# Moving one tile's layernorm statistics within VectorE's queue, in a two-layer graph network on one core

## The chip, the cores and the metric

The kernel runs on one core of a Trainium2 chip. The metric is the time on the device in microseconds, the median of three runs. The core has five engines that run their own instruction streams side by side: TensorE (PE, matrix products and transposes into PSUM), VectorE (DVE), ScalarE (ACT), GpSimd (POOL), and SyncE (SP), which issues the transfers. Each engine takes its instructions in the order in which they are written, and waits at an instruction until what it needs is ready.

## The reference, cut to what matters

There are 64 graphs of 256 nodes with 512 channels, and a 256 x 256 adjacency for each. Two layers follow one another, each on a normalised copy of x that passes through a relu, and each adds to x:

```python
h = jnp.maximum(_layernorm(x, axis=-1), 0.0)
# layer 0: attention with 8 heads of 64, masked by adj, and a gate
q, k, v = (x @ Wq.T, x @ Wk.T, x @ Wv.T)          # on h, split into heads
attn = softmax(where(adj != 0, q.k / 8, -inf))
c = attn @ v
gate = sigmoid(concatenate([c, h]) @ Wg.T + bg)
x = x + gate * h + (1.0 - gate) * c
h = jnp.maximum(_layernorm(x, axis=-1), 0.0)
# layer 1: graph attention with one head
Wh = h @ W
e = leaky_relu(Wh.a1[:, None] + Wh.a2[None, :], 0.2)
x = x + elu(softmax(where(adj == 0, -1e9, e)) @ Wh)
```

The statistics of the title are the mean and variance over the 512 channels of each node, for layer 0's layernorm.

## The kernel before, in words

**Tiles.** A graph's 256 nodes are two tiles of 128 rows, so x is one tile of 128 x 2 x 512 in float32, and t is 0 or 1 throughout. `norm_stats` (L186) takes the mean and variance of one row tile on VectorE: BATCH_NORM_STATS2 at L191, an aggregate at L192, and after the second tile an addition of epsilon at L195. GpSimd takes the power -1/2 (`norm_root`, L199), VectorE the bias (`norm_bias`, L203), ScalarE normalises (`norm_relu`, L208).

**Products.** All projections and the gate go through seven products of halves instead of eight (`strassen`, L153). Their sums are kept in three PSUM banks, a, b and c. Products 1 and 2 go to bank a; 6, 7 and 4 to b; 5 and 3 to c. Within a bank a product adds to what stands there. In between, the partial sum is read out: `u1` is a copy of bank a on ScalarE (L182); `u2` and `u3` are bank b plus u1 on VectorE (L180), after products 6 and 7; `c00`, `c10`, `c11` and `c01` are the four quarters of the result, of which c00 is ScalarE's and the others are VectorE's. Two facts of this bear on the change: product 4 adds to bank b, so it can't begin until u3 has read it; and the next family of products can't begin in bank b until c10 has read it. In the trace, product 1 of the gate begins with `pma_z<-hT_l,wgh_sb`, and product 4 is the group that begins with `pmb_z<-hT_l,wgh_t`.

**Rounds.** `emit_round(i)` (L607) writes the instructions of one round in a fixed order, by hand; nothing reorders them, and each engine keeps it. A round works on up to five graphs at once: attention of graph i, projections of p = i + 1, gate and layer 1's first half of q = i - 1, layer 1's second half of r = i - 2, and, ahead of these, the mask and statistics of p + 1. The load of x for p + 2 is issued at the end of a round (`load_graph`, L88), on SyncE's queue, after the store of graph r and the transfers of `p_send`; its statistics are taken in the next round, where that graph is p + 1.

**The stretch around the change** is the gate's. TensorE does products 1, 6, 5, two small transposes (`g_edges`, L529, which spread layer 1's edge terms over the rows, into `pe`), then products 7, 2, 4 and 3. VectorE does u2, the reciprocal of a softmax sum (L357), the statistics of tile 0, the logits (L535, two instructions, which read `pe`), the leaky relu (L542, one instruction that reads its tile twice), the row maximum (L544), u3, c11, block transposes of the attention weights (L370), the reciprocal of layer 1's sums (L558), the statistics of tile 1 with L195, c10, and then the gate's mix (`g_mix`, L453 and L455), which waits for ScalarE's tanh (L445), which waits for c10. ScalarE waits for the row maximum to take layer 1's exponential (L551), and then copies c00. GpSimd scales the attention weights (L361), takes the differences d for the gate (`g_diff`, L440, two subtractions), the sums for the projections' products (`p_sums`, L147 to L150) and the root (L199).

Of the kernel before, what the change touches and what calls it, by code (L numbers as in the profile page):

```python
# [22 lines left out]
def kernel(  # L23
# [79 lines left out]
    def weight_sums(key):  # L103

        w = weight[key]
        t = const.tile([P, 3, 2, w.shape[3]], F32, name=f"w{key}_t")
        b11, b12, b21, b22 = (w[:, r:r + 2, n, :] for r in (0, 2) for n in range(2))
        nc.vector.tensor_tensor(t[:, 1], b22, b12, ALU.subtract)
        nc.vector.tensor_tensor(t[:, 0], t[:, 1], b11, ALU.add)
        nc.vector.tensor_tensor(b12, b12, b11, ALU.subtract)  # L110
        nc.vector.tensor_tensor(t[:, 2], b21, t[:, 0], ALU.subtract)
        weight[key] = {1: b11, 2: b21, 3: b22, 4: t[:, 2], 5: b12, 6: t[:, 0], 7: t[:, 1]}
# [10 lines left out]
    def edge_columns():  # L123

        w = weight["1"]
        for c in range(HC):
            for side in range(2):
                scr = sb["tmp"].tile([P, 2, HH], F32, tag="t", name=f"scr_{c}_{side}")
                nc.vector.scalar_tensor_tensor(
                    scr, w[:, c, :, :HH], 1.0, a_sb[side].rearrange("p (n f) -> p n f", n=2),  # L130
                    ALU.mult, ALU.mult, accum_out=w[:, c, side, HH:],
                )
# [474 lines left out]
    def emit_round(i):  # L607


        p, q, r = i + 1, i - 1, i - 2  # L610

        def do(fn, g, *args):
            if 0 <= g < B:
                fn(g, *args)

        def run(fn, g, steps):
            if 0 <= g < B:
                if (fn, g) not in products:
                    products[fn, g] = fn(g)
                for step in steps.split():  # L620
                    products[fn, g](step)

        run(g_gate, q, "1")
        run(g_wh, r, "c01")
        do(a_turn, i, 0, 0)
        do(a_send, i, 0, 0)
        do(p_fetch, p)
        do(a_fetch, i, 0, 0)
        run(g_gate, q, "u1 6 u2 5")
        do(a_scale, i, 0, 1)  # L630
        do(p_stats, p + 1, 0)
        do(g_edges, r)
        do(g_logits, r)
        do(g_leaky, r)
        do(g_diff, q)
        run(g_gate, q, "7 u3 c11")
        do(g_exp, r)
        do(a_turn, i, 0, 1)
        do(a_send, i, 0, 1)
        do(a_fetch, i, 0, 1)  # L640
        run(g_gate, q, "2 c00")
        do(p_sums, p)
        do(g_rec, r)
        do(p_stats, p + 1, 1)
        do(p_root, p + 1)
        run(g_gate, q, "4 c10")
        do(g_tanh, q, 0)
        run(g_gate, q, "3")
        do(g_mix, q, 0, True)
        run(g_gate, q, "c01")  # L650
        do(g_tanh, q, 1)
        do(g_mix, q, 0, False)
        do(g_transpose, r)
        do(g_targets, r)
        do(p_mask, p + 1)
        do(g_mix, q, 1, True)
        do(g_mix, q, 1, False)
        do(g_turn, q)
        do(g_send, q)
        do(g_fetch, q)  # L660
        do(p_bias, p + 1)
        if i == -1:
            weight_sums("q")
            weight_sums("k")
        run(p_qk, p, "1 u1 6 5 u2")
        do(g_out, r, 0)
        do(g_neg, r, 0)
        do(g_pos, r, 0)
        do(a_scores, i, 1)
        do(a_weigh, i, 0)  # L670
        do(a_max, i, 1, 0)
        do(a_exp, i, 1, 0, 0)
        do(a_exp, i, 1, 0, 1)
        do(a_max, i, 1, 1)
        do(a_evac, i, 0)
        run(p_qk, p, "7")
        do(a_exp, i, 1, 1, 0)
        do(a_exp, i, 1, 1, 1)
        do(a_scale, i, 1, 0)
        run(p_qk, p, "u3")  # L680
        do(a_scale, i, 1, 1)
        run(p_qk, p, "c11 2 c00")
        do(a_turn, i, 1, 0)
        do(a_send, i, 1, 0)
        do(g_residual, q)
        do(a_fetch, i, 1, 0)
        run(p_qk, p, "4 c10")
        do(g_stats, q, 0)
        do(g_stats, q, 1)
        do(g_root, q)  # L690
        run(p_qk, p, "3 c01")
        if i == -1:
            weight_sums("v")
        run(p_v, p, "1 u1")
        do(g_bias, q)
        do(g_norm, q)
        run(p_v, p, "6 u2")
        do(g_elu, r, 0)
        do(g_add, r, 0)
        do(a_turn, i, 1, 1)  # L700
        do(a_send, i, 1, 1)
        do(a_fetch, i, 1, 1)
        do(g_out, r, 1)
        run(p_v, p, "5")
        do(g_neg, r, 1)
        if i == 0:
            weight_sums("gh")
            weight_sums("gc")
            nc.vector.tensor_scalar_mul(hbg, hbg, 0.5)
        run(p_v, p, "7 u3")  # L710
        do(g_transpose_h, q)
        run(p_v, p, "2")
        do(g_channels, q)
        run(p_v, p, "c11")
        do(g_sums, i)
        run(p_v, p, "c00")
        do(g_pos, r, 1)
        do(p_norm, p + 1)
        run(p_v, p, "4 c10 3 c01")
        do(g_elu, r, 1)  # L720
        do(g_add, r, 1)
        do(g_store, r)
        do(p_turn, p + 1)
        do(p_send, p + 1)
        do(load_graph, p + 2)
        if i == 0:
            edge_columns()
            weight_sums("1")
        run(g_wh, q, "1 u1 6 u2 5")
        do(a_scores, p, 0)  # L730
        do(a_max, p, 0, 0)
        do(a_exp, p, 0, 0, 0)
        do(a_exp, p, 0, 0, 1)
        run(g_wh, q, "7 2 c00")
        do(a_max, p, 0, 1)
        run(g_wh, q, "u3 c11")
        do(a_scale, p, 0, 0)
        do(a_exp, p, 0, 1, 0)
        do(a_weigh, i, 1)
        do(a_evac, i, 1)  # L740
        do(a_sums, i)
        do(a_exp, p, 0, 1, 1)
        run(g_wh, q, "4 c10 3")

    with tc.manual_schedule(engines={getattr(mybir.EngineType, e) for e in ("PE", "SP", "Pool", "DVE", "Activation")}):
        load_graph(0)
        load_weight("q", nc.sync)
        load_weight("k", nc.scalar)
        load_graph(1)
        load_weight("v", nc.sync)  # L750
        p_mask(0)
        p_stats(0, 0)
        p_stats(0, 1)
        for fn in (p_root, p_bias, p_norm, p_transpose_pe):
            fn(0)
        for i in range(-1, B + 2):
            if i == 0:
                load_weight("gh", nc.sync)
                load_weight("gc", nc.sync)
                load_weight("1", nc.sync)  # L760
                load_small()
            emit_round(i)
            graphs.pop(i - 2, None)
# [32 lines left out]
```

## Time and profile before

| what | value |
|---|---|
| time, median of three | 3369.89 us (3366.17 to 3376.53) |
| span of the profiled run | 3364.0 us, its time 3365.78 us |
| TensorE, busy with matmuls | 3262.3 us, 97% |
| VectorE busy | 2398.4 us, 71% |
| GpSimd busy | 1641.1 us, 49% |
| ScalarE busy | 1369.0 us, 41% |
| granted TensorE clock, mean | 0.991 |
| statistics L191 | 256 instructions, mean 675 ns; VectorE idle 85.9 us before them, for the load of x |

Half of the 256 statistics belong to layer 0, and half of those to tile 0. A line of a group in the page gives line, engine, operation, tiles written and read, shapes, count, then busy time, mean duration in ns, and the time that the engine sat idle ahead of it, with what ended that. A line of the list of waits gives who waited, for whom, the total in us, how often, and the longest. A line of a timeline gives start and duration in us, engine, line of the kernel, operation and tiles, and in brackets the idle time before it and what ended it. The work of a middle round repeats every 50.4 to 51.7 us.

### The profile page before, as it was taken

Reading aid. Unit: us, or ns where it says so; the run is one execution under the profiler, and the core shown is the slowest. Engines: PE = TensorE matmul, PEld = TensorE weight load, DVE = VectorE, ACT = ScalarE, POOL = GpSimd, SP = SyncE. Lnnn points to the kernel's source line nnn. Section 1 sums busy time; section 2 is a strip of 40 time slices with the busy share of each in tenths; the row PEclk is TensorE's granted clock in tenths of the full one; section 3 lists DMA queues with packets and bytes.
Section 4 is the critical chain, followed back from the end, with each engine's and each line's share of the span. In section 5 each row is a group of like instructions: output and inputs, shape, how many; then the busy total and the mean of one; then the engine's idle time right before and its main releaser. Section 6 shows DMA issues by size and latency. Waiting matters only on the chain. (4 is left out here: it accounts for less than half of the span.)

```text
span 3364.0 us, 66545 instructions
## 1 busy us (share of the span) xinstructions
PE 3262.3 (97%) x23448; PEld 2804.2 (83%) x23448; DVE 2398.4 (71%) x6245; ACT 1369.0 (41%) x3843; POOL 1641.1 (49%) x2439
## 2 busy tenths in 40 slices
PE   6999999999999999999999999999999999999996
PEld 5788888888888888888888888888888888888884
DVE  5777777777777776777777777777777777767764
ACT  2344443443443444343444434434444444434342
POOL 2454554544544544545545545445455445445453
PEclk8999999999999999999999999999999999999998
DMA  4455545545545545545545455455455455454541
GB/s 160 139 146 152 152 142 156 157 138 154 157 141 153 162 137 156 154 142 154 146 153 156 138 156 158 138 154 157 136 159 158 139 157 156 142 150 140 152 128 57
DMA packets 614765, 494.61 MB, mean 147 GB/s; under 512 B 291233, under 2 KB 540577, under 8 KB 614433
## 3 DMA queue, kind: packets, MB, share of 16 engines
q1 hardware_dynamic: 613376, 489.31, 49.4%
q8 instruction: 187, 3.06, 0.4%
q14 instruction: 146, 1.19, 0.1%
q10 hardware_dynamic: 1056, 1.05, 0.1%
HBM read 256.90 MB, written 233.31 MB: 146 GB/s over the span
## 5 line engine op out<-in xcount | busy, mean ns | idle before, releaser
L361 POOL TENSOR_SCALAR e<-e,rec 128x256 f32<-128x256 f32 x1024 | 471.4, 479 | 1104.6 <-DVE rec L357 640.4
L349 ACT ACTIVATE e<-e,low 128x256 f32<-128x256 f32 x1024 | 508.0, 499 | 201.9 <-DVE low L340 201.9
L340 DVE CUSTOM_DVE_ANT_0 e<-ps,mask 128x256 f32<-128x256 f32 x1024 | 363.3, 421 | 60.6 <-PE ps L325 60.2
L370 DVE STREAM_TRANSPOSE eb<-e 128x512 f32<-128x512 f32 x512 | 331.9, 686 | 3.5 <-POOL e L361 3.0
L325 PEld LDWEIGHTS ps<-qk 64*128 64x128 f32 x2048 | 187.8, 187 | 86.7 <-issue 69.3
L325 PE MATMUL ps<-qk 64*128 64x256 f32 x2048 | 256.5, 390 | 0.0
L402 PE MATMUL pc<-eT,v 128*64 128x256 f32 x2048 | 249.5, 386 | 0.3 <-DMA eT<-there_e 0.3
L577 PE MATMUL po<-wh,egT 128*128 128x512 f32 x512 | 245.0, 602 | 2.6 <-ACT egT L571 2.6
L551 ACT ACTIVATE eg<-eg,nm 128x256 f32<-128x256 f32 x128 | 64.0, 500 | 450.2 <-DVE nm L544 450.2
L191 DVE BATCH_NORM_STATS2 bs_l<-x 128x6 f32<-128x512 f32 x256 | 172.8, 675 | 85.9 <-DMA x<-in_x_dram 85.9
L208 ACT ACTIVATE h_l<-x,nb_l,rs_l 128x512 f32<-128x512 f32 x256 | 194.3, 808 | 61.8 <-DVE nb_l L203 46.0
L589 ACT ACTIVATE pos<-po,rec 128x512 f32<-128x512 f32 x128 | 88.3, 690 | 321.1 <-DVE neg L584 321.1
L402 PEld LDWEIGHTS pc<-eT,v 128*64 128x64 f32 x2048 | 135.7, 137 | 98.5 <-issue 22.4
L199 POOL TENSOR_TENSOR rs_l<-ve_l,mhalf 128x2 f32<-128x2 f32 x128 | 90.0, 703 | 261.1 <-DVE ve_l L195 258.8
L147 POOL TENSOR_TENSOR S_l<-hT_l 128x256 f32<-128x256 f32 x128 | 93.2, 728 | 238.8 <-ACT hT_l L136 162.4
L599 POOL TENSOR_TENSOR x<-x,pos 128x512 f32<-128x512 f32 x128 | 163.2, 1275 | 93.5 <-DVE pos L595 93.5
L445 ACT ACTIVATE z<-z,hbg 128x256 f32<-128x256 f32 x256 | 116.3, 501 | 222.3 <-DVE z L180 222.3
L349 ACT ACTIVATION_READ_ACCUMULATOR e<-e,low 128x1 f32 x1024 | 193.7, 189 | 0.0
L440 POOL TENSOR_TENSOR d<-hT_l,cT 128x512 f32<-128x512 f32 x128 | 174.5, 1384 | 0.0
L584 DVE TENSOR_SCALAR neg<-po,rec 128x512 f32<-128x512 f32 x128 | 93.4, 730 | 109.3 <-PE po L577 109.3
L180 DVE TENSOR_TENSOR u_qk<-pmb_qk,u_qk 128x512 f32<-128x512 f32 x128 | 87.8, 686 | 105.9 <-PE pmb_qk L169 105.9
L169 PEld LDWEIGHTS pmb_qk<-S_l,wq_t 128*128 128x128 f32 x1024 | 125.3, 193 | 33.5 <-issue 27.0
(144 smaller groups left out, 8235.7 us busy)
## 6 DMA issues: line engine op xcount, KB each, us to landing
there_e<-eb SPq DMA_DIRECT2D x256, 512.0 KB, 2.7
eT<-there_e SPq DMA_DIRECT2D x1024, 128.0 KB, 3.0
x<-in_x_dram SPq DMA_DIRECT2D x64, 512.0 KB, 5.8
out_dram<-x SPq DMA_DIRECT2D x64, 512.0 KB, 3.0
there_y<-y SPq DMA_DIRECT2D x63, 512.0 KB, 2.6
yT<-there_y SPq DMA_DIRECT2D x252, 128.0 KB, 3.0
there_h<-h_l SPq DMA_DIRECT2D x248, 128.0 KB, 3.6
hT_l<-there_h SPq DMA_DIRECT2D x248, 128.0 KB, 5.2
```

What stands on the lines that cost most here:

```text
L169: nc.tensor.matmul(bank[key][(slice(None), *cols)], lhsT, rhs, start=first and i == 0, stop=last and i == len(todo) - 1, skip_group_check= ...
L191: nc.vector.bn_stats(bs, s["x"][:, t, :])
L208: nc.scalar.activation(h[:, t, :], s["x"][:, t, :], AF.Relu, bias=s["nb"][:, t:t + 1], scale=s["rs"][:, t:t + 1])
L325: nc.tensor.matmul(psc[jj, i][:, t, :], qk[r:r + DK, 0, jj, t * P:(t + 1) * P], qk[r:r + DK, 1, jj, :], start=True, stop=True,)
L340: nc.vector.tensor_tensor_reduce(s["e", half, jj][:, i, t, :], s["ps", half][jj, i][:, t, :], s["mask"][:, t, :], -SCALE, HUGE, ALU.add, A ...
L349: nc.scalar.activation(e, e, AF.Exp, bias=s["low", half][:, jj, i, t:t + 1], scale=-1.0, accum_out=s["sums", half][:, jj, i, t:t + 1],)
L361: nc.gpsimd.tensor_scalar(e, e, rec[:, i, t:t + 1], 1.0, ALU.mult, ALU.mult)
L370: nc.vector.transpose(eb[:, :, 4 * i:4 * i + 4, :].rearrange("p b n c -> p n b c"), e[:, i])
L402: nc.tensor.matmul(pc[i * DK:(i + 1) * DK, jj, :].rearrange("p (t a c) -> p t a c", t=NT, c=32), s["v"][:, kc, hd * DK:(hd + 1) * DK], eT[ ...
L440: nc.gpsimd.tensor_tensor(d, s["hT"][:, :, js, :], s["cT"][:, :, js, :], ALU.subtract)
L577: nc.tensor.matmul(pm, s["egT"][:, kc, t * P:(t + 1) * P], s["wh"][:, kc, :, :HH], start=(kc == 0), stop=(kc == NT - 1))
L599: nc.gpsimd.tensor_tensor(s["x"][:, t, :], s["x"][:, t, :], s.pop(("pos", t)), ALU.add)
```

## The change

Within `emit_round` two things change their place, and with them their place in VectorE's queue. The statistics of tile 0 of graph p + 1 stood behind the scaling's reciprocal and ahead of the logits; now they stand behind the block transposes, c00 and layer 1's reciprocal. The gate's `4 c10` stood behind both tiles' statistics and the root; now it stands between the two tiles' statistics. No instruction is added, dropped or altered. Its purpose is that VectorE should not stand before the load of x while the logits and u3 are queued behind it.

```diff
         run(g_gate, q, "u1 6 u2 5")
         do(a_scale, i, 0, 1)
-        do(p_stats, p + 1, 0)
         do(g_edges, r)
         do(g_logits, r)
         do(g_leaky, r)
...
         run(g_gate, q, "2 c00")
         do(p_sums, p)
         do(g_rec, r)
+        do(p_stats, p + 1, 0)
+        run(g_gate, q, "4 c10")
         do(p_stats, p + 1, 1)
         do(p_root, p + 1)
-        run(g_gate, q, "4 c10")
         do(g_tanh, q, 0)
         run(g_gate, q, "3")
         do(g_mix, q, 0, True)
```

## The prediction

> **What bounds the kernel now.** I read the page's table of engines first, then TensorE's list of waits, then the timelines of one long and one short round.
>
> ```profile
> PE 3262.3 (97%) x23448; PEld 2804.2 (83%) x23448; DVE 2398.4 (71%) x6245; ACT 1369.0 (41%) x3843; POOL 1641.1 (49%) x2439
> ...
> L542 DVE SCALAR_TENSOR_TENSOR eg<-eg 128x512 f32<-128x512 f32 x64 | 77.2, 1206 | 2.2
> ```
>
> TensorE has work during 97% of the span, so only what still makes it wait can be won. The second line is put by for later: L542 has a mean of 1206 ns, while the same kind of instruction on the same shape takes 697 ns at L453. The waits of TensorE, with total, count and longest:
>
> ```profile
> PE pmb_z L169 <- DVE u_z L180: 34.8, 31, 2.8
> PE pt_l L268 <- ACT h_l L208: 23.6, 6, 11.7
> PE pmb_z L169 <- POOL S_c L148: 8.1, 1, 8.1
> PE pmb_qk L169 <- POOL S_l L148: 6.3, 1, 6.3
> ```
>
> The last three rows are start and end of the program (few waits, long ones). The first is the only wait of the steady state: 31 of some 60 rounds. The timeline says which u_z it is. First a long round, 51.65 us from one start of the gate's step 1 to the next, that starts at 1523.37 (VectorE, then TensorE, then GpSimd; columns are start, duration, instruction, idle time before it and what ended that):
>
> ```profile
> 1527.20 0.42 DVE L180 TENSOR_TENSOR u_z<-pmb_z,u_z 128x256 f32<-128x256 f32 x1 [1.99 <-issue]
> ...
> 1529.25 0.69 DVE L191 BATCH_NORM_STATS2 bs_l<-x 128x6 f32<-128x512 f32 x1 [1.54 <-DMA x<-in_x_dram]
> ...
> 1530.07 0.84 DVE L535 SCALAR_TENSOR_TENSOR eg<-pe,wh,mask 128x256 f32<-128x256 f32 x2
> 1530.95 1.70 DVE L542 SCALAR_TENSOR_TENSOR eg<-eg 128x512 f32<-128x512 f32 x1
> 1532.69 0.69 DVE L544 TENSOR_REDUCE nm<-eg 128x2 f32<-128x512 f32 x1
> 1533.29 0.41 DVE L180 TENSOR_TENSOR u_z<-pmb_z,u_z 128x256 f32<-128x256 f32 x1
> ```
>
> ```profile
> 1528.73 0.38 PE L529 MATMUL pe<-ident,wh 128*128 128x128 f32 x2
> ...
> 1533.76 1.16 PE L169 MATMUL pmb_z<-hT_l,wgh_t 128*128 128x128 f32 x8 [1.08 <-DVE u_z L180]
> ```
>
> ```profile
> 1529.61 2.50 POOL L440 TENSOR_TENSOR d<-hT_l,cT 128x512 f32<-128x512 f32 x2
> ```
>
> Then a short round, 50.41 us, that starts at 2797.71:
>
> ```profile
> 2802.53 0.69 DVE L191 BATCH_NORM_STATS2 bs_l<-x 128x6 f32<-128x512 f32 x1 [0.49 <-DMA x<-in_x_dram]
> ...
> 2803.49 0.87 DVE L535 SCALAR_TENSOR_TENSOR eg<-pe,wh,mask 128x256 f32<-128x256 f32 x2
> 2804.39 1.37 DVE L542 SCALAR_TENSOR_TENSOR eg<-eg 128x512 f32<-128x512 f32 x1
> ...
> 2806.40 0.41 DVE L180 TENSOR_TENSOR u_z<-pmb_z,u_z 128x256 f32<-128x256 f32 x1
> ```
>
> The reader is to see a chain. The statistics of x (tile 0) wait for the load of x; behind them in VectorE's queue stand the logits, the leaky step L542, the maximum, and then u3, which must read bank b before step 4 may accumulate into it. All further times are counted from the start of step 1 of the round. u3 begins at 9.92 in the long round and at 8.69 in the short one. TensorE reaches step 4 at 9.16 and u3 takes 0.41, so 8.69 is just in time and 9.92 is 1.08 us of idle TensorE.
>
> Between the two rounds nothing else differs on this path, and the delay comes in a **step, not in proportion**: over rounds 1 to 60, L542 that starts at 7.38 or earlier ends at 8.05 to 8.08 (29 rounds), one that starts from 7.45 to 8.36 ends at 9.28 or 9.29 in all but one. Whatever begins in between waits for an edge. GpSimd's two subtractions of L440 run from 6.24 to 7.51 and from 7.47 to 8.74, and these are the edges: L542 takes its 0.69 us in the seam between them, or after the second.
>
> **What the Trainium skill says.** "SBUF — State Buffer", section "Who interferes with whom": a VectorE instruction with two SBUF inputs contends with a GpSimd instruction that reads SBUF, and the shared port pair is held as an exclusive lock for a whole instruction. L542 has two SBUF inputs and L440 reads SBUF; 0.69 us free against up to 1.84 us beside L440 agrees. "Perfetto Trace Analysis", section "Identifying the Most-Contended Engine": busy share of matmuls is a poor measure of the distance to the bound; here too the list of waits told more than the 97%. "TensorE: Matmul & The Clock Gate", section "What's actually happening": a free-running activity window of about 3.4 us decides on half or full clock, and an idle one halves it. In the trace one 3.41 us stretch at half clock begins 0.2 us after the longest wait, and no other in the middle of the program; that wait was 2.75 us, so less than a whole window was enough.
>
> **The change part by part.**
>
> Nothing is added or dropped: 63 BATCH_NORM_STATS2 (0.67 us) and 63 aggregates (0.18 us) of tile 0 move within VectorE's queue, from ahead of the logits to behind the block transposes, c00 and the reciprocal; and c10 moves ahead of the statistics of tile 1.
>
> *Removed ahead of u3.* Two things: the wait for x (85.9 us over 59 waits, mean 1.46) and 0.67 + 0.18 us of work. What then bounds the logits is pe, the two transposes at L529, which end at 5.74 (1529.11 - 1523.37). So logits at 5.78, L542 at 6.69, in every round. This case is in the trace already: rounds 61 and 62 have no statistics of a later graph, their logits start at 5.78, L542 at 6.69 and takes 1.36, and u3 comes at 8.69. L542 at 6.69 lies inside the first subtraction of L440 and well ahead of the 7.4 where the step is, with 0.7 us to spare. Hence u3 at 8.69 always, and no wait at step 4.
>
> *What that is worth.* A long round costs 51.65 - 50.42 = 1.23 us more: 1.08 of wait and 0.15 of restart. 31 waits give 34.8 us, the restarts 31 x 0.15 = 4.7, and the one long wait with its half clock a further 54.95 - 50.42 - 2.75 - 0.15 = 1.6. Sum 41.1; adding up what each of the rounds 1 to 60 has over 50.42 gives 41.0, so I take **41 us**.
>
> *Added behind.* In a short round of before the reciprocal L558 ends at 10.82, then statistics of tile 1, aggregate and the epsilon add L195 (0.17 to 0.45), then c10 from 12.00 to 12.41. After: statistics and aggregate of tile 0 end at about 11.62, c10 runs from 11.66 to 12.07, 0.35 earlier. Step 4 has ended by 11.0, so c10 doesn't wait for it. tanh follows c10 by 0.1 and takes 0.91 for its two: to 13.08. Meanwhile VectorE does tile 1's 0.67 + 0.18 and L195, to 13.1 or 13.4. The mix d (L453) began at 13.51 before, after 1.10 us in which VectorE waited for tanh; that idle time hides the statistics. So the cost is **nothing**, bounded by 0 and by 0.4 us of VectorE that TensorE doesn't wait for.
>
> *The waits that move.* The wait for x stands now at about 10.75. In the trace x came at 8.56 at the latest, so I take zero. Behind it queue c10 (tanh waits for it; so does p_qk's step 6 for bank b, at 15.05, 3 us after c10's end) and, from there on, work for which TensorE shows no wait. GpSimd's root rs_l waits for L195 and moves from 12.2-14.1 to about 13.3; GpSimd's next work behind it is the next scaling, well past 20, and VectorE needs the root (L203) at about 18. The block transposes and their send come no later than in a short round.
>
> **The rivals.**
>
> *A, the forecast:* all rounds short. 3365.8 for the profiled run less 41.0 = 3324.8. The median of before is 4 us above the profiled run, which I put down to some more long rounds; these go too, and I leave 1 us for odd rounds like number 32 (0.37 us). **3326.**
>
> *B, half stays:* u3 at 8.69 leaves no slack (its end at 9.10, step 4 at 9.16). If the lock at L542 or a slip of the later pieces brought the step back in half of the rounds, 3369.9 - 20 = 3350. For it speaks that the margin at step 4 is 0.06 us; against it rounds 44 to 47, four short ones in a row, and rounds 61 and 62.
>
> *C, the wait only changes its place:* c10 or the mix late, bank b or c free late for the projections of q and k. It would take over 3 us at c10 to touch p_qk; then about 3367. Against it: the earlier c10 worked out above.
>
> *D, slower:* the 0.85 us of tile 0 lands whole on the path in its new place, 60 x 0.87 = 52 us against 41 won: 3381. It would need TensorE to wait for d, c01 or y; no row of before has such a wait, and 1.10 us of VectorE idle time stands right there.
>
> **How the numbers follow.** A 0.87, B 0.05, C 0.04, D 0.04. The time is A's. The low end is the floor of 3324.8 less the 0.1% by which runs scatter; the high end takes in B's milder half, a quarter of the loss left with a slow run: 3345. Faster by over 0.3% (below 3359.8): A and B, 0.92; within: C, 0.04; slower: D, 0.04.
>
> **What would show it.** Right: no row of TensorE waiting for u_z at step 4, or a few; VectorE's wait for x gone from L191; logits waiting some 1.4 us for pe instead (1.44 in rounds 61 and 62); L542 near 1.36 us in all middle rounds; rounds at 50.42; d's wait for tanh down from 1.10 to below 0.3 us. Wrong: L542 near 1.7 with u3 at 9.9, a new row of TensorE waiting for z or y, or L191 still waiting for x at its new place.

## The result, and the profile after

The changed kernel takes 3322.99 us (median of four runs, 3321.47 to 3324.14), against 3372.3 us before (3366.17 to 3376.53, four runs; the 3369.89 of the table above is the median of the first three). The ratio is 0.9855, with a 95% interval of 0.9837 to 0.9872: 1.45% faster. The runs also lie closer together, within 2.7 us where the kernel before spread over 10.

The row of the statistics in the page of the kernel before, and then the engines and the same row in the page of the changed kernel:

```profile
L191 DVE BATCH_NORM_STATS2 bs_l<-x 128x6 f32<-128x512 f32 x256 | 172.8, 675 | 85.9 <-DMA x<-in_x_dram 85.9
```

```profile
PE 3255.3 (98%) x23448; PEld 2803.0 (84%) x23448; DVE 2405.5 (72%) x6245; ACT 1369.6 (41%) x3843; POOL 1674.8 (50%) x2439
...
L191 DVE BATCH_NORM_STATS2 bs_l<-x 128x6 f32<-128x512 f32 x256 | 172.2, 673 | 0.0
```

Behind the second bar stands VectorE's idle time ahead of the statistics: 85.9 us before, none now. TensorE's waits, longest in total first:

```profile
PE pt_l L268 <- ACT h_l L208: 23.9, 6, 11.7
PE pmb_z L169 <- POOL S_c L148: 8.3, 1, 8.3
PE pmb_qk L169 <- POOL S_l L148: 6.3, 1, 6.3
```

The row of 34.8 us for u_z is gone, and no new one of that kind has come; what is left belongs to the start and the end. VectorE waits elsewhere, where it costs nothing. One row of before, then two of now:

```profile
DVE d L453 <- ACT z L445: 63.2, 59, 1.5
```

```profile
DVE eg L535 <- PE pe L529: 91.4, 64, 1.5
...
DVE d L453 <- ACT z L445: 5.0, 7, 1.1
```

The logits now wait for pe, 91.4 us in total, about as long as VectorE used to wait for x; the mix waits 5.0 us for tanh in place of 63.2. One middle round of the changed kernel, whose step 1 of the gate starts at 1507.84, VectorE and then TensorE at step 4:

```profile
1513.62 0.88 DVE L535 SCALAR_TENSOR_TENSOR eg<-pe,wh,mask 128x256 f32<-128x256 f32 x2 [1.44 <-PE pe L529]
1514.53 1.37 DVE L542 SCALAR_TENSOR_TENSOR eg<-eg 128x512 f32<-128x512 f32 x1
...
1516.54 0.41 DVE L180 TENSOR_TENSOR u_z<-pmb_z,u_z 128x256 f32<-128x256 f32 x1
...
1518.59 0.67 DVE L191 BATCH_NORM_STATS2 bs_l<-x 128x6 f32<-128x512 f32 x1
...
1519.39 0.39 DVE L180 TENSOR_TENSOR z<-pmb_z,u_z 128x256 f32<-128x256 f32 x1
...
1521.23 0.68 DVE L453 SCALAR_TENSOR_TENSOR d<-z,d 128x512 f32<-128x512 f32 x1
```

```profile
1517.00 1.16 PE L169 MATMUL pmb_z<-hT_l,wgh_t 128*128 128x128 f32 x8
```

The first of the two L180 is u3, the second is c10. L542 begins at 6.69 after the start of the round and u3 at 8.70, as in the short rounds of before, and step 4 has no idle time ahead of it. All of the rounds 1 to 60 are as long as this one: their lengths lie between 50.41 and 50.42 us. Before, the same 60 had a mean of 51.10. The difference is 60 x 0.687 = 41.2 us, of the 41.8 us by which the span of the profiled run fell (3364.0 to 3322.2); the other 0.6 lies outside these rounds.

### The profile page after: what moved, and what is told of

It is laid out like the page before. It is cut to its first block, busy times and chain, and to the rows that moved or that the text cites. A ratio compares the mean times of both kernels' runs of the same rounds, so it can differ in the third digit from the quotient of the medians.

```text
span 3322.2 us, 66546 instructions
## 1 busy us (share of the span) xinstructions
PE 3255.3 (98%) x23448; PEld 2803.0 (84%) x23448; DVE 2405.5 (72%) x6245; ACT 1369.6 (41%) x3843; POOL 1674.8 (50%) x2439
## 5 line engine op out<-in xcount | busy, mean ns | idle before, releaser
L402 PE MATMUL pc<-eT,v 128*64 128x256 f32 x2048 | 249.5, 385 | 0.4 <-DMA eT<-there_e 0.4
L199 POOL TENSOR_TENSOR rs_l<-ve_l,mhalf 128x2 f32<-128x2 f32 x128 | 104.9, 820 | 271.6 <-DVE ve_l L195 268.9
L589 ACT ACTIVATE pos<-po,rec 128x512 f32<-128x512 f32 x128 | 88.4, 690 | 337.6 <-DVE neg L584 337.6
L402 PEld LDWEIGHTS pc<-eT,v 128*64 128x64 f32 x2048 | 135.6, 136 | 98.6 <-issue 22.5
L440 POOL TENSOR_TENSOR d<-hT_l,cT 128x512 f32<-128x512 f32 x128 | 188.0, 1490 | 0.0
L584 DVE TENSOR_SCALAR neg<-po,rec 128x512 f32<-128x512 f32 x128 | 93.4, 730 | 125.1 <-PE po L577 125.1
L180 DVE TENSOR_TENSOR u_qk<-pmb_qk,u_qk 128x512 f32<-128x512 f32 x128 | 87.8, 686 | 105.5 <-PE pmb_qk L169 105.5
```

Source lines behind the costliest of these rows:

```text
L402: nc.tensor.matmul(pc[i * DK:(i + 1) * DK, jj, :].rearrange("p (t a c) -> p t a c", t=NT, c=32), s["v"][:, kc, hd * DK:(hd + 1) * DK], eT[ ...
L440: nc.gpsimd.tensor_tensor(d, s["hT"][:, :, js, :], s["cT"][:, :, js, :], ALU.subtract)
```

## The experiments

The numbers in brackets behind a time are its lowest and highest run, those behind a ratio its 95% interval. Each ratio is to the kernel before, run on the same chip. Times within a round are counted from the start of the gate's step 1, as in the prediction.

**The two parts of the change, one at a time.** Statistics alone, against the kernel before:

```diff
-        do(p_stats, p + 1, 0)
         do(g_edges, r)
...
         do(g_rec, r)
+        do(p_stats, p + 1, 0)
         do(p_stats, p + 1, 1)
         do(p_root, p + 1)
         run(g_gate, q, "4 c10")
```

> Only the statistics of tile 0 move; c10 stays behind both tiles' statistics and the root. Theory (the wait for x and its 0.85 us of work stood ahead of u3, and everything else is slack): as fast as the changed kernel, 3323 us, rounds of 50.42 us; c10 begins 0.85 us later than before, at about 12.9 after step 1 of the gate, and the mix at about 14.3, and TensorE has no wait for either. Rival (the earlier c10 has a part in the gain): slower than the changed kernel by over 10 us, with a row of TensorE waiting for z or y.

3323.82 us (3320.54 to 3329.11), ratio 0.9872 (0.9857 to 0.9887). The whole gain is there, within the scatter of the runs. One middle round of this run, which starts at 1506.93:

```profile
1519.93 0.41 DVE L180 TENSOR_TENSOR z<-pmb_z,u_z 128x256 f32<-128x256 f32 x1
1521.44 0.69 DVE L453 SCALAR_TENSOR_TENSOR d<-z,d 128x512 f32<-128x512 f32 x1 [1.10 <-ACT z L445]
```

c10 at 13.00 is 1.45 us later than in the changed kernel's round above (11.55) and the mix at 14.51 is 1.12 us later (13.39), and the wait for tanh is back, but TensorE waits for neither. c10 alone, against the kernel before:

```diff
         do(g_rec, r)
+        run(g_gate, q, "4 c10")
         do(p_stats, p + 1, 1)
         do(p_root, p + 1)
-        run(g_gate, q, "4 c10")
```

> Only c10 moves ahead of the statistics of tile 1; tile 0's statistics stay ahead of the logits. Theory: nothing is won, 3370 us, TensorE still waits for u3 in about half of the rounds. Rival (c10 has a part in the gain): 3340 to 3360 us.

3366.78 us (3360.18 to 3377.45), ratio 1.0008 (0.9995 to 1.0020). TensorE still waits for u3 in the profiled run:

```profile
PE pmb_z L169 <- DVE u_z L180: 43.1, 36, 2.5
```

The move of c10 alone gains nothing.

**The wait without the work.** The changed kernel with one small reader of x in the old place:

```diff
+    def touch(g):
+        one = st.tile([P, 1], F32, tag="one", name=f"one_{g}")
+        nc.vector.tensor_copy(one, graphs[g]["x"][:, 0, 0:1])
...
+        do(touch, p + 1)
         do(g_edges, r)
```

> The changed kernel, with one more instruction of VectorE in the old place, which copies one column of x of tile 0 (128x1): the wait for x is back ahead of the logits, without the 0.85 us of statistics. Theory (wait and work together push L542 past the edge at 7.4): L542 passes it only where x comes after about 6.4, which is 7 of 60 rounds of the kernel before, so 10 to 12 us above the changed kernel, about 3334 us. Rival 1 (the wait alone is the whole loss): back at 3370 us. Rival 2 (the work alone): 3323 us.

3331.37 us (3330.40 to 3332.55), ratio 0.9893 (0.9878 to 0.9908): 8 us above the changed kernel, a little less than forecast. Only 4 of 60 rounds of its profiled run are long ones, those in which the reader began at 6.61 or later. So the wait alone makes only a small part of the loss, a sixth by the medians. The share is no fixed figure: in this run the reader began at 5.58 in the mean, where the statistics of before began at 5.77, so x came a little earlier.

**The work without the wait.** Fillers in the old place of the changed kernel: three, four or five statistics of an x that has long been there, whose results nothing reads:

```diff
+    def filler(g, count):
+        for k in range(count):
+            bs = st.tile([P, 6], F32, tag="bf", name=f"bf_{g}_{k}")
+            nc.vector.bn_stats(bs, graphs[g]["x"][:, 0, :])
...
+        do(filler, i, 3)
         do(g_edges, r)
```

> The changed kernel, with three more BATCH_NORM_STATS2 over an x that has long been loaded, into a buffer that nothing reads, in the place where tile 0's statistics stood: some 1.8 us of work, no wait for a transfer. Theory (work is hidden while the logits wait for pe, and then by the first subtraction of L440): the work runs from 4.3 to about 6.0, L542 begins near 6.9, ends at 8.05, no cost: 3323 us. Rival (what moved away was paid for by its work): 60 rounds x 0.85 us or more, over 3370 us.

> The same with four: work until about 6.6, L542 near 7.5, just past the edge. Theory of the lock: L542 ends at 9.28 in every round, each round 51.65 us, so 3323 + 62 x 1.23 = 3399 us. Rival (no lock): u3 moves by what the work is longer, about 0.2 us past 8.69 and 0.15 for the restart, so 3345 us or less.

> The same with five: work until about 7.2, L542 near 8.1, still inside the second subtraction. Theory of the lock: no dearer than four, 3399 us. Rival (no lock): 0.6 us a round more than with four, some 36 us above it.

Three: 3323.82 us (3323.11 to 3325.35). Four: 3400.30 us (3399.21 to 3402.92). Five: 3400.02 us (3398.33 to 3402.61). Three together cost less than 1 us, the fourth 76 us, the fifth nothing more. A middle round with four, which starts at 1540.26 (VectorE, then GpSimd), and one with five, which starts at 1541.48:

```profile
1544.51 2.44 DVE L610 BATCH_NORM_STATS2 bf<-x 128x6 f32<-128x512 f32 x4
...
1547.77 1.78 DVE L542 SCALAR_TENSOR_TENSOR eg<-eg 128x512 f32<-128x512 f32 x1
...
1550.19 0.41 DVE L180 TENSOR_TENSOR u_z<-pmb_z,u_z 128x256 f32<-128x256 f32 x1
```

```profile
1546.50 2.50 POOL L440 TENSOR_TENSOR d<-hT_l,cT 128x512 f32<-128x512 f32 x2
```

```profile
1545.73 3.03 DVE L610 BATCH_NORM_STATS2 bf<-x 128x6 f32<-128x512 f32 x5
...
1549.58 1.20 DVE L542 SCALAR_TENSOR_TENSOR eg<-eg 128x512 f32<-128x512 f32 x1
...
1551.41 0.41 DVE L180 TENSOR_TENSOR u_z<-pmb_z,u_z 128x256 f32<-128x256 f32 x1
```

L542 begins at 7.50 with four and at 8.10 with five, and ends at 9.29 in both, half a microsecond after the second subtraction of L440 (8.74 with four): the extra 0.6 us of work comes off the time for which it is held. u3 comes at 9.93 in both. With three L542 begins at 6.91 and takes 1.16 us, and all 60 middle rounds are at 50.43 to 50.44.

**Whose lock it is.** GpSimd's two subtractions L440 moved out of L542's way, in the kernel before (the edit shown), and in the changed kernel with five fillers:

```diff
+        do(g_diff, q)
         do(a_scale, i, 0, 1)
...
         do(g_leaky, r)
-        do(g_diff, q)
```

> The kernel before, with GpSimd's two subtractions L440 ahead of its scaling, in a stretch where GpSimd stood idle, so that nothing of GpSimd with two inputs runs beside L542; the statistics of tile 0 stay ahead of the logits. Theory (L542 is held by L440, which makes a step of a small delay): L542 takes 0.69 us in all rounds, each late round loses only what x is late past 5.69, which sums to 17 us over the 31 rounds of before, with restarts 22; so 3350 to 3354 us, and about as many waits of TensorE but of unequal length. Rival (no lock, the delay is VectorE's own work): 3370 us, L542 still at up to 1.8 us.

> Five more statistics as before, and GpSimd's subtractions L440 ahead of its scaling. Theory of the lock: L542 takes 0.69 us and begins near 8.1, u3 near 9.45, TensorE waits some 0.6 us and 0.15 for the restart, 62 rounds: 3323 + 47 = 3370 us, so 29 us faster than with five alone. Rival (L440 is not what holds L542): the same as with five alone.

Kernel before: 3342.27 us (3339.88 to 3345.44), ratio 0.9923 (0.9906 to 0.9940). L542, with shortest, median and longest duration in ns, and TensorE's wait for u3:

```profile
L542 DVE SCALAR_TENSOR_TENSOR eg<-eg x64: 691/692/694, 152.8 to 3324.9; 128x512 f32<-128x512 f32 x64
```

```profile
PE pmb_z L169 <- DVE u_z L180: 16.4, 26, 1.8
```

The step is gone, and a late x now costs in proportion: statistics that start at 6.16 give a round of 50.93 us, statistics that start at 6.92 one of 51.68. The sum was less well foreseen, and the time lies below the range given. The middle rounds lose 22.1 us over 50.42, the 22 of the theory, but by chance: x came later than in the kernel before (VectorE waits 93.0 us for it, not 85.9), and the rounds without a wait are shorter, 50.30, so that the loss over these is 29.2 us. That moving L440 would shorten even the short rounds was not foreseen; the part on the changed kernel's bound, below, comes back to it. The range was also counted down from the median of before, which lies above the profiled run of before; counted up from 3323, the 22 us give 3345.

With five fillers: 3370.67 us (3369.09 to 3372.50), ratio 0.9998 (0.9988 to 1.0009). It is 29 us faster than with five fillers and L440 in its place. A middle round, which starts at 1528.86 (VectorE, then GpSimd):

```profile
1536.06 0.86 DVE L535 SCALAR_TENSOR_TENSOR eg<-pe,wh,mask 128x256 f32<-128x256 f32 x2
1536.95 0.69 DVE L542 SCALAR_TENSOR_TENSOR eg<-eg 128x512 f32<-128x512 f32 x1
```

```profile
1530.93 2.50 POOL L440 TENSOR_TENSOR d<-hT_l,cT 128x512 f32<-128x512 f32 x2
```

L542 begins at 8.10, as above, and takes 0.69 us. So it is L440 that held it, although L542 reads nothing that L440 writes, and the step in the loss is L440's edge. The runs show who holds whom and until when; what inside the chip is held they do not show.

**Is the changed kernel at its bound?** The same move of L440 in the changed kernel:

> The changed kernel, with L440 ahead of the scaling as well. Theory (TensorE has no wait left in the middle, so a faster L542 buys nothing): 3323 us; L542 falls from 1.37 to 0.69 us, u3 comes near 8.0 and step 4 stays at 9.16. Rival (the lock still costs something in the changed kernel): faster than 3323 us by more than its interval.

3317.88 us (3317.47 to 3318.05), ratio 0.9842 (0.9821 to 0.9862). The theory failed here: the time is 5 us below the changed kernel's. The round that starts at 1503.85, at step 4:

```profile
1513.00 1.06 PE L169 MATMUL pmb_z<-hT_l,wgh_t 128*128 128x128 f32 x8
```

The eight matmuls take 1.06 us here and 1.16 in the changed kernel. Laid against one another instruction by instruction, the two rounds differ at one place: the second matmul of step 4 comes 0.12 us sooner, the first taking 275 ns in place of 377. The rounds have a mean of 50.30 us in place of 50.42, and 60 x 0.114 = 6.8 us, which the change in span (3322.2 to 3315.7) bears out. In the changed kernel u3 is thus still late by a hair in every round, so little that no wait is shown. The kernel before with L440 moved shows the same within one run: in the 18 middle rounds in which u3 began at 8.58 or earlier, that first matmul took 275 to 277 ns; in the three with u3 at 8.66 or 8.67 it took 357 to 373, and 377 in the other 39. By these figures this version is faster than both kernels. Its median and the changed kernel's were measured at different times, and the intervals of their ratios to the kernel before overlap; the lengths of the rounds are what shows the difference.

**How much room is behind c10?** Fillers in the changed kernel directly ahead of c10, three and then six (the edit shown):

```diff
         do(p_stats, p + 1, 0)
+        do(filler, i, 6)
         run(g_gate, q, "4 c10")
```

> The changed kernel, with three more BATCH_NORM_STATS2 directly ahead of c10, over an x that has long been loaded, into a buffer that nothing reads: c10 and the mix come 1.8 us later, c10 from about 13.4. Theory (c10 has about 3 us before product 6 of the projections of q and k, at 15.05, needs bank b): no cost, 3323 us. Rival (the mix behind c10 has less slack than that): slower, with a new wait of TensorE.

> The same with six: c10 from about 15.15 to 15.55. Theory: product 6 of q and k waits for c10 some 0.55 us and 0.15 for the restart, 62 rounds: 3323 + 43 = 3366 us, with a row of TensorE at pmb_qk waiting for z. Rival (the slack at c10 is larger than 3 us): 3323 us.

Three: 3325.93 us (3325.04 to 3326.14); 3 us more than the changed kernel, where none were expected. The middle rounds are at 50.43; of the 2.1 us by which the span of the profiled run is longer, 1.0 lies in them and the rest outside. Six: 3404.08 us (3401.60 to 3405.78), 81 us more than the changed kernel, not 43. A middle round, which starts at 1541.14:

```profile
1556.79 1.13 PE L169 MATMUL pmb_qk<-S_l,wq_t 128*128 128x128 f32 x8 [0.42 <-DVE z L180]
...
1558.87 1.16 PE L169 MATMUL pmc_qk<-S_l,wq_sb 128*128 128x128 f32 x8
...
1564.74 1.52 PE L402 MATMUL pc<-eT,v 128*64 128x256 f32 x12 [0.18 <-ACT pos L589]
```

Against the changed kernel this round falls back three times: by 0.66 us at product 6, which waits for c10 as the theory said; by 0.32 at product 5, which needs bank c and c01; and by 0.25 at L402, which waits for L589. The last is the third step of a chain: VectorE reached L584 at 22.03 in place of 20.56, with no idle time ahead of it where it had waited 1.72 us before, and ScalarE's L589 needs it. The 0.66 us alone would give 60 x 0.66 = 40 us, about the 43 expected. So the slack at c10 is the 3 us that the prediction gave, but c10 is not all that stands behind the fillers.

## Why the prediction was right

*The bound and the chain.* Right: TensorE's only recurring wait of the middle rounds was the one for u3 at step 4, and it has gone. That it was the statistics and not c10 is shown by moving each alone. That the wait and the work made the loss together is shown too: the wait alone costs 8 us, work of 1.8 us alone nothing.

*The lock that makes a step of it.* Right, and shown by the fillers: 1, 77 and 77 us above the changed kernel for three, four and five. Moving L440 turned the step into a loss in proportion.

*The worth of 41 us.* Right in the profiled run, where the middle rounds gained 41.2. The median fell by more, 49 us; the profiled run of before was faster than all four runs of the result. The prediction took the 4 us between the profiled run and its median for more of the same loss. The run with c10 alone, whose statistics stand in the old place, agrees: in its profiled run VectorE waits 98.7 us for x in place of 85.9, the middle rounds lose 50.1 us in place of 41.0, and the time is 3374.61 in place of 3365.78. Why x comes later in one run than in another stays open. The prediction gave 3326, or 3324.8 for the profiled run without the 1 us for odd rounds; that run took 3323.97. No odd round came.

*The cost behind.* Right: over the middle rounds c10 began at 11.54 to 11.55, a tenth sooner than forecast, and the mix at 13.04 to 13.44, against 13.51 in the short round read before. GpSimd's root began at 13.03 to 15.58, in some rounds later than the 13.3 forecast, and took 945 ns in the mean where it had taken 708; VectorE's wait for it has not grown (19.2 us in total, 19.8 before). The earlier c10 was more than was needed: with c10 left behind both statistics the time is the same. Rivals C and D did not come: TensorE has no new row of waits for z, d or y.

*Where it was off.* "8.69 is just in time" was wrong by a tenth: u3 at 8.69 still holds step 4 back by about 0.12 us, in the short rounds of before too. So 50.42 us is no floor, and rival B's point, that there is no slack at step 4, holds in small: 7 us remain to be won in the changed kernel. They do not touch the forecast, because the 50.42 from which it was counted contained them. And the "0.15 of restart" is not a restart. A wait in the list counts from the modelled end of the last matmul; matmuls of this shape start every 112 ns and are shown as lasting 275, so an idle time is shown about 0.16 us too short. Laid against the changed kernel, a long round falls back by 1.227 us in one step at step 4, of which 1.078 is shown as idle. The sum was right all the same, because it was made from the lengths of rounds.

Two smaller readings did not hold, and changed nothing. Step 4 ends at 11.21 in the short round read, not by 11.0, still ahead of c10 at 11.55. L195 takes 0.17 to 0.74 us in the changed kernel, not 0.17 to 0.45.

## What to carry to other kernels

In an engine's fixed order, an instruction that waits for a transfer should stand behind those that release the engine that sets the pace. In this kernel its exact new place hardly mattered; but count the slack for all that is queued behind it, as the six fillers show. When rounds fall into short and long ones with a sharp edge between, look for a lock, or for long instructions on another engine: set the end of the delayed instruction against its start. A wait that has vanished from the list can still cost a tenth of a microsecond per round; compare the lengths of rounds with a version in which the releaser comes much earlier.

## What the runs showed of the hardware

When L542 begins during the first L440, it runs at the seam between the two: in the changed kernel's middle rounds it begins at 6.69, the first L440 ends at 7.50, and L542 ends at 8.05. The second L440 is then the one that waits, with a duration of 1.73 us in place of the 1.27 of the long rounds of before. A first matmul of a group takes 377 ns instead of 275 when what releases it comes only just in time, with no idle time shown ahead of it.

The length of a wait of TensorE alone does not decide whether its clock is halved. Besides the wait of 2.75 us that the prediction read, a wait of 2.51 us (c10 alone) and one of 1.82 us (kernel before with L440 moved) were each followed within 1.1 us by 3.41 us at half clock; waits of 2.33 and 1.68 us in the run with c10 alone were not.
